# The first batch element of a graph network on one core: its loads over three queues, y plus x on VectorE, layer three's weights folded sooner

## The chip, the cores and the metric

The kernel runs on one core of one Trainium2 chip. The metric is the device time of one execution in microseconds (us). The time before is 2398.67 us, the median of three runs (2397.93 to 2399.6).

The engines have short names in the profile: PE is TensorE (PEld its weight loads), DVE is VectorE, ACT is ScalarE, POOL is GpSimd and SP is SyncE, which here only starts transfers. Each engine takes its instructions in its own order and waits at the first one that isn't ready.

## The reference

Sixteen batch elements, each with 1024 nodes of 128 features (`x`) and a dense 1024 x 1024 matrix `adj`. Layer 0 is applied first, then a network of four message layers, each time with a residual and a layer norm:

```python
# layer 0
degree = adjacency_matrix.sum(axis=-1)[:, :, None]
sum_neighbors = jnp.einsum('bid,bij->bjd', embeddings, cost_matrix) / degree
out = jnp.einsum('bnk,dk->bnd', concatenate([embeddings, sum_neighbors]), W) + b
x = _layernorm(x + relu(out))
# one of the four message layers
src_agg = jnp.einsum('bjv,bij->biv', nodes @ ws + bs, _l2norm(adj, 2))
dst_agg = jnp.einsum('bjv,bji->biv', nodes @ wd + bd, _l2norm(adj, 1))
upd = jnp.concatenate([src_agg, nodes @ wn + bn, dst_agg], axis=2)
nodes = jnp.tanh(upd @ wu + bu)
# after the four layers
x = _layernorm(x + nodes)
```

Both matrices of layer 0 are `adj`. Layers three and four also take the stashed results of earlier layers. `_l2norm` divides the rows (2) or the columns (1) of the matrix by their root of summed squares.

## The kernel before, in words

The order of every engine is written out by hand in the source (a manual schedule over the five engines); a loop over the batch elements holds the layers, and small functions called between the products of a layer (its hooks, numbered by the product that they stand ahead of) prepare what comes next. While one element is computed, the next one's matrix is loaded and its layer 0 computed alongside. The first element has no predecessor, so its loads and its layer 0 stand ahead of the loop, in an order of their own. The change edits only this part and the hooks of the first element's first message layer.

The first element goes as follows. Names and lines are those of the kernel before.

- *Loads.* `load_nodes` (L1056) brings one half of x in four transfers, `load_pair` (L1052) two of the eight row blocks of the matrix, 1 MB, in four transfers (one for each group of 32 partitions). SP takes groups 0 and 1 and GpSimd groups 2 and 3, x first, then the four pairs in the order of `PAIRS`; half 1 of the rows comes ahead of half 0. `w0n` and `b0c` are layer 0's weights and bias. `fetch_weights` (L187 to L192) brings a message layer's three weight matrices `ws`, `wd`, `wn`, its update matrix `wu` and four bias vectors; `load_rows` (L640) brings the matrix once more, in quarters by rows, for the transposed copy `at`. All of these are issued by SP. The order is: weights of layers one and two, row quarter 2, layer three, row quarter 3, layer four, row quarters 0 and 1.
- *Layer 0.* `to_xT` transposes x (L1094), `weights_of_x` multiplies it with W's first half (L1154), and `with_x` (L1163) starts the sum y + x in PSUM with a product of x and the identity. For each row block ScalarE forms squares (`square`, L1114), VectorE the row sum (`degree`, L1120) and TensorE two gather products (`gather`, L1127); GpSimd adds the squares up (`add_square`, L1117). `degree_row` turns the inverse degrees into a row (`dinv`, L359 and L1147), `scaled` (L1150) divides by them, `weights_of_agT` (L1157) finishes y, ScalarE applies the relu (L1158), and `with_y` (L1169) adds y to the sum in PSUM. `norm_stats` (L470 to L481) forms mean and variance on VectorE and the power `rs` on GpSimd; `norm_write_act` and `norm_write` (L490, L486) write x1, and `to_x1` (L1174, L1175) transposes it.
- *Weights.* The update matrix is multiplied into the message weights. `fold_begin` transposes the three matrices (L205, copies L206) and forms the biases (L209, L211, copies L215 to L218); `fold_end` forms the products (L227, copies L229 and L230). Layers one and two are folded inside layer 0, layers three and four by hooks of the first message layer: layer three at hooks 5 and 8, with sums of its weights (L148 to L155) in hook 11.
- *First message layer.* `messages` forms the products of x1 (`pt`, L247) with their additions on VectorE (L698); `row_factors0` forms the row factors `rinv`, and ScalarE scales the row quarters by them (L647); VectorE transposes these into `at` (L655), and `cinv0` makes the row of column factors `cinv` (L359, L351), by which `scale_columns` (L414) scales the matrix. `plain_layer` runs the products `z` and `d` (L851).

TensorE multiplies float32 in two passes: a product in the source is two matmuls in the profile; a transpose is one.

Of the kernel before, what the change touches and what calls it, by code (L numbers as in the profile page):

```python
# [14 lines left out]
P = 128  # L15
NL = 4
CHUNKS = [1, 1, 2, 3]
G = 4
# [5 lines left out]
def adj_resnorm_kernel(ctx: ExitStack, tc: tile.TileContext, x, adj, w0, b0, layers, out):  # L24
# [152 lines left out]

        return wm if l in PAIRED else wm[:, :KEPT[l] * 2 * P].rearrange("p (c v) -> p c v", v=2 * P)

    def fetch_weights(raw, l, q, wm=None):  # L180
        ws, bs, wd, bd, wn, bn, wu, bu = layers[l]
        nch = CHUNKS[l]
        size = max(3 * nch * P, KEPT[l] * 2 * P, WIDTH[l])
        flat = raw.take(size) if wm is None else wm[:, WIDTH[l]:]
        wr = flat[:, :3 * nch * P].rearrange("p (k c v) -> p k c v", k=3, c=nch)
        for k, w in enumerate((ws, wd, wn)):
            q.dma_start(wr[:, k], w.rearrange("(c p) v -> p c v", p=P))  # L187
        wur = raw.take(3 * P).rearrange("p (k v) -> p k v", k=3)
        q.dma_start(wur, wu.rearrange("(c p) v -> p c v", p=P))
        bc = raw.take(4)  # L190
        for k, v in enumerate((bs, bd, bn, bu)):
            q.dma_start(bc[:, k:k + 1], v.rearrange("(p o) -> p o", o=1))  # L192
# [48 lines left out]
    def small(name, shape=(K,)):  # L241
        return ps_s.tile([P, *shape], F32, tag="small", name=name)
# [806 lines left out]
    def load_pair(q, pair, groups):  # L1049
        h, k = pair  # L1050
        for g in groups:
            q.dma_start(a[g * C:(g + 1) * C, h * BPH + k:h * BPH + k + 2], av[h][g, :, k:k + 2])  # L1052

    def load_nodes(q, h, groups):
        for g in groups:
            q.dma_start(xn[g * C:(g + 1) * C, h * BPH:(h + 1) * BPH], xv[h][g])  # L1056

    nc.sync.dma_start(w0n, w0)
    shares = ((nc.sync, range(G // 2)), (nc.gpsimd, range(G // 2, G)))
    for h in (1, 0):  # L1060
        for q, groups in shares:
            load_nodes(q, h, groups)
    make_identity(nc, ident)
    for pair in PAIRS:
        for q, groups in shares:
            load_pair(q, pair, groups)
    nc.sync.dma_start(b0c, b0.rearrange("(p o) -> p o", o=1))
# [29 lines left out]
    pt = small("w0tr", [HW])  # L1097
    for k in range(2):
        nc.tensor.transpose(pt[:, k * P:(k + 1) * P], w0n[:, k * P:(k + 1) * P], ident)
    nc.scalar.copy(w0T.rearrange("p k v -> p (k v)"), pt[:, :2 * P])  # L1100

    sq = []
    for p in (3, 4):
# [9 lines left out]
    def square(i):  # L1113
        nc.scalar.activation(sq[i], a[:, i, :], AF.Square, accum_out=cols[:, i:i + 1])  # L1114

    def add_square(i):
        nc.gpsimd.tensor_add(sq[4], sq[4], sq[i])  # L1117
# [53 lines left out]
    def to_x1(h):  # L1171
        pt = product(f"x1tr_{h}")
# [11 lines left out]
    nc.vector.tensor_add(sq[6], sq[6], sq[7])  # L1184
    add_square(5)
    add_square(6)
# [26 lines left out]
    fold_end(0, fetched[0])  # L1213
    stats[0] = norm_stats(pn[0], range(BPH), "0_0_0")
    root_inverses(cols, inv, slice(NB))
    add_square(second)
    biases = fold_begin(1, fetched[1], nc.vector.tensor_copy, True)
    for q in range(BPH):
        norm_write_act(x1n[:, BPH + q], pn[1][:, q], stats[1], q)
# [17 lines left out]
    for b in range(B):  # L1237
# [8 lines left out]
        if b == 0:  # L1246
# [4 lines left out]
                for q in (2, 3):  # L1251
                    scale_rows(rows[q], q, rinv)

            t = messages(b, 0, feats, wm, {0: lambda: to_x1(0), 2: row_factors0}, with_sums=False)
            cinv = {}

            def columns0(rows, h, engine=nc.vector):
# [2 lines left out]
            def rows0(destination, finish):  # L1260
                for q in (2, 3):
                    transpose_rows(rows[q], q, at)

            def cinv0(destination, finish):
                cinv[0] = factor_rows_now(0, 1, inv, "cinv")

            def second0(destination, finish):
                columns0(range(NJ, NB), 1)
                sums_of_weights(2, fetched[2][3])
                weight_sums(own_seven(2, fetched[2][3]))  # L1270
                nc.sync.dma_start(wsave[2], fetched[2][3])
                destination(1, cinv[0])
                columns0(range(NJ), 1)

# [19 lines left out]
            def folded(l, part):  # L1294
                return lambda *_: part(l, fetched[l])

            hooks = {4: lambda *_: inverses(0, st0, NB), 5: folded(2, fold_begin), 6: rows0, 7: cinv0,
                     8: folded(2, fold_end), 9: lambda *_: fold_and_scale(3, 0), 11: second0, 12: folded(3, fold_end),
                     14: lambda *_: scale_rows(rows[1], 1, rinv), 18: first0, 26: sums0}
            T = combined(0, "T")  # L1300
            plain_layer(b, 0, feats, t, wm, a, at, f1, "acc", hooks)
# [353 lines left out]
```

## Time and profile before

| | |
|---|---|
| median of three runs | 2398.67 us (2397.93 to 2399.6) |
| the profiled execution's own time | 2397.22 us |
| its span, first to last instruction | 2395.3 us |
| TensorE busy | 2377.4 us, 99% of the span |
| VectorE busy | 2088.5 us, 87% |
| ScalarE busy | 977.2 us, 41% |
| GpSimd busy | 273.8 us, 11% |
| moved by DMA | 232.02 MB, 97 GB/s on average |
| granted TensorE clock | 0.999 of full speed |

A profile shows one execution. The time of a run lies 1.9 us above the span here, for what comes before the first and after the last instruction. Busy shares are averages over the whole span; for a change to one stretch the timeline of that stretch is read. It lists, for each engine, when a run of like instructions starts, how long it is busy, the line of the source, the operation with its output and inputs by the program's names, and in brackets how long the engine had been idle and what ended that. "issue" there means that nothing in the profile ended it; at a matmul it can be a transfer.

### The profile page before, as it was taken

Reading aid. Unit: us, or ns where it says so; the run is one execution under the profiler, and the core shown is the slowest. Engines: PE = TensorE matmul, PEld = TensorE weight load, DVE = VectorE, ACT = ScalarE, POOL = GpSimd, SP = SyncE. Lnnn points to the kernel's source line nnn. Section 1 sums busy time; section 2 is a strip of 40 time slices with the busy share of each in tenths; the row PEclk is TensorE's granted clock in tenths of the full one; section 3 lists DMA queues with packets and bytes.
Section 4 is the critical chain, followed back from the end, with each engine's and each line's share of the span. In section 5 each row is a group of like instructions: output and inputs, shape, how many; then the busy total and the mean of one; then the engine's idle time right before and its main releaser. Section 6 shows DMA issues by size and latency. Waiting matters only on the chain.

```text
span 2395.3 us, 39279 instructions
## 1 busy us (share of the span) xinstructions
PE 2377.4 (99%) x15293; PEld 1195.3 (50%) x15293; DVE 2088.5 (87%) x2799; ACT 977.2 (41%) x1827; POOL 273.8 (11%) x102
## 2 busy tenths in 40 slices
PE   8999999999999999999999999999999999999998
PEld 4444464454645446454454554546445464554644
DVE  5998888989889989889988889888898988998954
ACT  5524344253343534435244452434425344352322
POOL 4101111001111011110111110111100111101110
PEclk9999999999999999999999999999999999999999
DMA  9527344262533627235272443624427253362400
GB/s 201 128 75 147 69 114 90 71 147 57 138 75 81 137 48 160 58 97 115 55 163 57 106 97 71 147 69 109 93 69 151 57 133 77 79 142 48 100 22 22
DMA packets 365897, 232.02 MB, mean 97 GB/s; under 512 B 152785, under 2 KB 336849, under 8 KB 365713
## 3 DMA queue, kind: packets, MB, share of 16 engines
q1 hardware_dynamic: 364944, 227.16, 42.5%
q0 software_dynamic: 768, 2.36, 0.4%
q8 instruction: 121, 1.98, 0.4%
q14 instruction: 64, 0.52, 0.1%
HBM read 209.59 MB, written 19.84 MB: 96 GB/s over the span
## 4 chain that ended last, share of the span: by engine, by line
PE 95%; DVE 2%; DMA 1%; SPq 1%; issue 0%; ACT 0%; POOLq 0%; DVEq 0%; ACTq 0%
PE m L1005 39%; PE z L1005 29%; PE pt L247 9%; PE m_f L583 5%; PE pt_z L247 5%; PE z_f L583 2%; PE pw L247 2%; PE m3s L1005 1%; PE z L851 1%; DMA wm<-in_L_gnn_ws_dram 1%; PE pt_p L247 1%; SPq L640 0%; DVE acc L331 0%; DMA raw<-in_L_gnn_wu_dram 0%; DMA a<-in_adj_dram 0%
## 5 line engine op out<-in xcount | busy, mean ns | idle before, releaser
L1005 PE MATMUL m<-a,t 128*64 128x512 f32 x1008 | 432.3, 593 | 0.2 <-DVE t L711 0.2
L1005 PE MATMUL m<-at,t 128*64 128x512 f32 x1008 | 417.3, 593 | 0.0
L1005 PE MATMUL m<-Q,S 128*64 128x512 f32 x880 | 394.0, 593 | 0.0
L1005 PE MATMUL m<-T,S 128*64 128x512 f32 (+1 forms) x1040 | 393.0, 573 | 0.0
L456 POOL TENSOR_TENSOR rs<-ve,mhalf 128x32 f32<-128x32 f32 x30 | 191.9, 6395 | 987.9 <-DVE ve L454 987.9
L1005 PE MATMUL z<-at,t 128*64 128x512 f32 x504 | 229.2, 592 | 0.0
L1005 PE MATMUL z<-at,S 128*64 128x512 f32 x504 | 228.3, 593 | 0.0
L1005 PE MATMUL z<-a,S 128*64 128x512 f32 x504 | 228.2, 593 | 0.0
L1005 PE MATMUL z<-a,t 128*64 128x512 f32 x504 | 227.2, 593 | 0.0
L1005 PE MATMUL z<-Q,t 128*64 128x512 f32 x504 | 227.0, 593 | 0.0
L1005 PEld LDWEIGHTS m<-T,S 128*64 128x64 f32 x1040 | 134.2, 137 | 127.9 <-issue 121.5
L1005 PEld LDWEIGHTS m<-a,t 128*64 128x64 f32 x1008 | 133.6, 137 | 123.5 <-issue 110.9
L1005 PEld LDWEIGHTS m<-at,t 128*64 128x64 f32 x1008 | 135.9, 137 | 112.6 <-issue 107.5
L1005 PEld LDWEIGHTS m<-Q,S 128*64 128x64 f32 x880 | 118.2, 137 | 121.8 <-issue 118.6
L884 ACT COPY e<-m 64x512 f32<-64x512 f32 x63 | 36.6, 581 | 335.9 <-PE m L1005 335.5
L1005 PE MATMUL z<-T,t 128*64 128x512 f32 x384 | 172.8, 592 | 0.0
L376 POOL TENSOR_TENSOR inv<-cols,mhalf 128x16 f32<-128x16 f32 (+1 forms) x17 | 46.8, 2751 | 1031.9 <-DVE cols L375 1031.9
L414 DVE TENSOR_TENSOR a<-a,cinv 128x512 f32<-128x512 f32 x250 | 154.1, 692 | 1.6 <-ACT cinv L351 1.3
L322 ACT ACTIVATE sq<-a 128x1024 f32<-128x1024 f32 x120 | 125.9, 1050 | 35.9 <-DVE acc L329 22.5
L247 PE MATMUL pt<-wm,f1T 128*64 128x128 f32 (+1 forms) x1536 | 126.0, 309 | 0.0
L317 ACT ACTIVATE a<-a 128x1024 f32<-128x1024 f32 x120 | 125.2, 1045 | 0.4
L247 PEld LDWEIGHTS pt<-wm,f1T 128*64 128x64 f32 x1536 | 100.0, 137 | 39.2 <-issue 18.7
(300 smaller groups left out, 4891.9 us busy)
## 6 DMA issues: line engine op xcount, KB each, us to landing
a<-in_adj_dram SPq DMA_DIRECT2D x120, 512.0 KB, 12.9
rows<-in_adj_dram SPq DMA_DIRECT2D x480, 64.0 KB, 2.2
a<-in_adj_dram SPq DMA_DIRECT2D x240, 128.0 KB, 3.5
wm<-wsave SPq DMA_DIRECT2D x32, 704.0 KB, 5.0
wm<-wsave SPq DMA_DIRECT2D x31, 320.0 KB, 3.3
xn<-in_x_dram SPq DMA_DIRECT2D x124, 64.0 KB, 5.5
xs<-in_x_dram SPq DMA_DIRECT2D x60, 128.0 KB, 3.6
cinv<-dr SPq DMA_DIRECT2D x30, 256.0 KB, 6.3
```

What stands on the lines that cost most here:

```text
L247: nc.tensor.matmul(out[s], x[:, s], y, start=start, stop=stop)
L317: nc.scalar.activation(a[:, i, :], a[:, i, :], AF.Copy, accum_out=degree)
L322: nc.scalar.activation(sq, a[:, i, :], AF.Square, accum_out=state["cols"][:, i:i + 1])
L376: nc.gpsimd.tensor_tensor(inv[:, s], cols[:, s], mhalf[:, s], ALU.pow)
L414: engine.tensor_mul(a[:, i, s], a[:, i, s], cinv[:, s])
L456: nc.gpsimd.tensor_tensor(rstd, ve, mhalf[:, :n], ALU.pow)
L583: nc.tensor.matmul(o, x_, y_, start=start, stop=stop)
L851: nc.tensor.matmul(nodes(o) if len(y.shape) == 4 else o, x_, y, start=start, stop=stop)
L884: nc.scalar.copy(e0[high], A[high])
L1005: nc.tensor.matmul(o, x, y_, start=start, stop=stop)
```

## The change

Six things are edited, all in the first element:

- x is loaded by ScalarE's queue, half 1 first and half 0 behind two blocks of the matrix; the four pairs of row blocks are spread over SP, GpSimd and ScalarE; `w0n` follows SP's first two blocks. All bias vectors, `b0c` and those of the four message layers, are loaded by GpSimd's queue (`qb`).
- VectorE clears a tile `idle`, and TensorE forms three products of zeros with it ahead of everything else.
- The transposes of x and W and the products with x stand between the gathers instead of ahead of them.
- y is transposed into PSUM and VectorE adds x to it, into `x1n`, which the norm then reads and writes in place; before, four products added y to a product of x and the identity.
- The weights of layer three are loaded ahead of row quarter 2 instead of behind it (those of layer four ahead of quarter 3); `fold_begin` of layer three stands ahead of the loop, `fold_end` between the message products, and the sums of its weights in hook 6.
- x1's first half is transposed after layer two's fold instead of ahead of it, and the second square of the last pair is formed after the second half of y.

The edits word for word, shortened where lines only move:

```diff
-            q.dma_start(bc[:, k:k + 1], v.rearrange("(p o) -> p o", o=1))
+            (qb or q).dma_start(bc[:, k:k + 1], v.rearrange("(p o) -> p o", o=1))
...
+    idle = one.tile([P, HW], F32, tag="S2", name="idle")
+    nc.vector.memset(idle, 0.0)
+    load_nodes(nc.scalar, 1)
+    load_pair(nc.sync, 0, (0, 1))
+    load_pair(nc.gpsimd, 0, (2,))
+    make_identity(nc, ident)
+    load_pair(nc.scalar, 0, (3,))
     nc.sync.dma_start(w0n, w0)
-    shares = ((nc.sync, range(G // 2)), (nc.gpsimd, range(G // 2, G)))
-    for h in (1, 0):
-        for q, groups in shares:
-            load_nodes(q, h, groups)
-    make_identity(nc, ident)
-    for pair in PAIRS:
-        for q, groups in shares:
-            load_pair(q, pair, groups)
-    nc.sync.dma_start(b0c, b0.rearrange("(p o) -> p o", o=1))
+    load_pair(nc.gpsimd, 1, (2, 3))
+    load_pair(nc.sync, 1, (0,))
+    load_pair(nc.scalar, 1, (1,))
+    load_nodes(nc.scalar, 0)
+    load_pair(nc.scalar, 2, (3,))
+    load_pair(nc.gpsimd, 2, (1, 2))
+    load_pair(nc.sync, 2, (0,))
+    load_pair(nc.gpsimd, 3, (2,))
+    load_pair(nc.scalar, 3, (3,))
+    load_pair(nc.sync, 3, (0, 1))
+    nc.gpsimd.dma_start(b0c, b0.rearrange("(p o) -> p o", o=1))
...
-    for l, q in enumerate((None, 2, 3, None)):
-        fetched.append(fetch_weights(raw, l, nc.sync, None if l else wm))
+    for l, q in enumerate((None, None, 2, 3)):
+        fetched.append(fetch_weights(raw, l, nc.sync, None if l else wm, nc.gpsimd))
...
+    pt = product("idle")
+    for _ in range(3):
+        nc.tensor.matmul(pt, idle[:, :P], idle, start=True, stop=True)
...
     def with_x(h):
-        pn[h] = ps_t.tile([P, BPH, P], F32, tag="pt", name=f"yn0_{h}")
-        nc.tensor.matmul(pn[h].rearrange("p q d -> p (q d)"), ident, xn[:, h * BPH:(h + 1) * BPH].rearrange("p q d -> p (q d)"),
-                         start=True, stop=False)
-    def with_y(h):
+        pt = ps_t.tile([P, BPH, P], F32, tag="pt", name=f"yn0_{h}")
         for q in range(BPH):
             i = h * BPH + q
-            nc.tensor.matmul(pn[h][:, q], yT[:, i * P:(i + 1) * P], ident, start=False, stop=q == BPH - 1)
+            nc.tensor.transpose(pt[:, q], yT[:, i * P:(i + 1) * P], ident)
+        pn[h] = x1n[:, h * BPH:(h + 1) * BPH]
+        nc.vector.tensor_add(pn[h], pt, xn[:, h * BPH:(h + 1) * BPH])
...
-    for h in (1, 0):
-        to_xT(h)
-        with_x(h)
-        weights_of_x(h)
-    for pair in PAIRS[:2]:
-        squares_of(*pair)
-        gathers_of(*pair)
+    to_xT(1)
+    squares_of(*PAIRS[0])
+    gathers_of(*PAIRS[0])
+    transposes_of_w0()
+    squares_of(*PAIRS[1])
+    gathers_of(*PAIRS[1])
+    weights_of_x(1)
+    to_xT(0)
...
     squares_of(*PAIRS[2])
     gathers_of(*PAIRS[2])
+    weights_of_x(0)
...
     square(first)
-    square(second)
     gather(0, second)
     add_square(first)
-    with_y(1)
     scaled(0)
+    with_x(1)
     weights_of_agT(0)
     stats = {1: norm_stats(pn[1], range(BPH), "0_0_1", True)}
+    square(second)
     fold_begin(0, fetched[0])
-    with_y(0)
+    with_x(0)
...
-    to_x1(1)
     biases()
     fold_end(1, fetched[1])
+    to_x1(1)
     for q in range(BPH):
-        norm_write(x1n[:, q], pn[0][:, q], stats[0], q)
+        norm_write(pn[0][:, q], pn[0][:, q], stats[0], q)
+    fold_begin(2, fetched[2])
...
+            def second_x1():
+                to_x1(0)
+                fold_end(2, fetched[2])
...
             def rows0(destination, finish):
                 for q in (2, 3):
                     transpose_rows(rows[q], q, at)
+                sums_of_weights(2, fetched[2][3])
+                weight_sums(own_seven(2, fetched[2][3]))
+                nc.sync.dma_start(wsave[2], fetched[2][3])
```

More of the change, by code (lines that the diff above doesn't have):

```diff
@@ L178, in as_chunks, with fetch_weights @@
         return wm if l in PAIRED else wm[:, :KEPT[l] * 2 * P].rearrange("p (c v) -> p c v", v=2 * P)
-    def fetch_weights(raw, l, q, wm=None):
+    def fetch_weights(raw, l, q, wm=None, qb=None):
         ws, bs, wd, bd, wn, bn, wu, bu = layers[l]
@@ L1047, in adj_resnorm_kernel, with load_pair, load_nodes @@
     PAIRS = [(h, k) for h in (1, 0) for k in range(0, BPH, 2)]
-    def load_pair(q, pair, groups):
-        h, k = pair
+    def load_pair(q, i, groups):
+        h, k = PAIRS[i]
         for g in groups:
             q.dma_start(a[g * C:(g + 1) * C, h * BPH + k:h * BPH + k + 2], av[h][g, :, k:k + 2])
-    def load_nodes(q, h, groups):
-        for g in groups:
+    def load_nodes(q, h):
+        for g in range(G):
             q.dma_start(xn[g * C:(g + 1) * C, h * BPH:(h + 1) * BPH], xv[h][g])
-    nc.sync.dma_start(w0n, w0)
-    shares = ((nc.sync, range(G // 2)), (nc.gpsimd, range(G // 2, G)))
-    for h in (1, 0):
-        for q, groups in shares:
-            load_nodes(q, h, groups)
-    make_identity(nc, ident)
-    for pair in PAIRS:
-        for q, groups in shares:
-            load_pair(q, pair, groups)
-    nc.sync.dma_start(b0c, b0.rearrange("(p o) -> p o", o=1))
+    idle = one.tile([P, HW], F32, tag="S2", name="idle")
[5 more added lines that the diff above has]
+    load_pair(nc.scalar, 0, (3,))
+    nc.sync.dma_start(w0n, w0)
+    load_pair(nc.gpsimd, 1, (2, 3))
[9 more added lines that the diff above has]
+    nc.gpsimd.dma_start(b0c, b0.rearrange("(p o) -> p o", o=1))
     raw = Raw()
@@ L1095, in to_xT, with transposes_of_w0 @@
         nc.scalar.copy(nodes(xT[:, half(h)]), blocks(pt))
[L1097 to L1100, printed above, removed]
+    pt = product("idle")
+    for _ in range(3):
+        nc.tensor.matmul(pt, idle[:, :P], idle, start=True, stop=True)
+    def transposes_of_w0():
+        pt = small("w0tr", [HW])
+        for k in range(2):
+            nc.tensor.transpose(pt[:, k * P:(k + 1) * P], w0n[:, k * P:(k + 1) * P], ident)
+        nc.scalar.copy(w0T.rearrange("p k v -> p (k v)"), pt[:, :2 * P])
     sq = []
@@ L1218, in adj_resnorm_kernel @@
     for q in range(BPH):
-        norm_write_act(x1n[:, BPH + q], pn[1][:, q], stats[1], q)
-    to_x1(1)
+        norm_write_act(pn[1][:, q], pn[1][:, q], stats[1], q)
     biases()
     fold_end(1, fetched[1])
+    to_x1(1)
     for q in range(BPH):
-        norm_write(x1n[:, q], pn[0][:, q], stats[0], q)
+        norm_write(pn[0][:, q], pn[0][:, q], stats[0], q)
+    fold_begin(2, fetched[2])
     kept = scratch.tile([N, D], F32, tag="kept", name="kept0")
@@ L1252, in row_factors0 @@
                     scale_rows(rows[q], q, rinv)
-            t = messages(b, 0, feats, wm, {0: lambda: to_x1(0), 2: row_factors0}, with_sums=False)
+            def second_x1():
+                to_x1(0)
+                fold_end(2, fetched[2])
+            t = messages(b, 0, feats, wm, {0: second_x1, 2: row_factors0}, with_sums=False)
             cinv = {}
@@ L1268, in second0 @@
                 columns0(range(NJ, NB), 1)
-                sums_of_weights(2, fetched[2][3])
-                weight_sums(own_seven(2, fetched[2][3]))
-                nc.sync.dma_start(wsave[2], fetched[2][3])
                 destination(1, cinv[0])
@@ L1295, in folded @@
                 return lambda *_: part(l, fetched[l])
-            hooks = {4: lambda *_: inverses(0, st0, NB), 5: folded(2, fold_begin), 6: rows0, 7: cinv0,
-                     8: folded(2, fold_end), 9: lambda *_: fold_and_scale(3, 0), 11: second0, 12: folded(3, fold_end),
+            hooks = {4: lambda *_: inverses(0, st0, NB), 6: rows0, 7: cinv0,
+                     9: lambda *_: fold_and_scale(3, 0), 11: second0, 12: folded(3, fold_end),
                      14: lambda *_: scale_rows(rows[1], 1, rinv), 18: first0, 26: sums0}
```

## The prediction

> **What bounds the kernel now.** I read the page first, for the share that the change can reach. Two lines carry it:
>
> ```profile
> span 2395.3 us, 39279 instructions
> ...
> PE   8999999999999999999999999999999999999998
> ```
>
> The row PE gives TensorE's busy share in 40 slices of 59.9 us. Only the first and the last slice hold idle TensorE time; the change edits the first element, which is the first slice. All it can win is what TensorE loses there, and what follows is shifted as a whole. So I read that slice instruction by instruction in the timeline (start, duration, engine, line, operation, and in brackets the idle time before it and what ended it).
>
> ```profile
> 13.28 0.30 PEld L1127 LDWEIGHTS pa<-a,xn 128*128 128x128 f32 x2 [2.90 <-issue]
> 13.29 1.06 ACT L1114 ACTIVATE sq<-a 128x1024 f32<-128x1024 f32 x1 [3.26 <-DMA a<-in_adj_dram]
> 13.30 2.35 DVE L1120 TENSOR_REDUCE cols<-a 128x1 f32<-128x1024 f32 x2 [8.20 <-DMA a<-in_adj_dram]
> ...
> 18.87 1.22 DVE L1184 TENSOR_TENSOR sq<-sq,sq_row 128x1024 f32<-128x1024 f32 x1
> ...
> 20.00 0.17 DVE L1124 RECIPROCAL inv<-cols 128x4 f32<-128x4 f32 x1
> ...
> 20.29 0.41 PEld L359 LDWEIGHTS dinv<-ident,inv 128*128 128x128 f32 x4 [0.70 <-issue]
> ```
>
> TensorE, ScalarE and VectorE all start on the matrix at 13.3 us, when the first pair of row blocks (1 MB) has landed. From there the gathers run at 0.43 us a pass, 16 passes for two pairs, and the third pair waits at 20.29 for a chain that ends on ScalarE: squares, sum of two squares on VectorE, reciprocal, transposes (`dinv`). The same view of GpSimd:
>
> ```profile
> 8.41 0.53 POOL L1052 DMA_DIRECT2D a<-in_adj_dram  x1 [0.50 <-DMA xn<-in_x_dram]
> ...
> 15.57 2.36 POOL L1117 TENSOR_TENSOR sq<-sq,sq 128x1024 f32<-128x1024 f32 x1 [6.51 <-ACT sq L1114]
> 20.24 2.37 POOL L1117 TENSOR_TENSOR sq<-sq,sq 128x1024 f32<-128x1024 f32 x1 [2.31 <-DVE inv L1124]
> 22.75 2.37 POOL L1117 TENSOR_TENSOR sq<-sq,sq_x 128x1024 f32<-128x1024 f32 x1
> ...
> 30.15 2.35 POOL L1117 TENSOR_TENSOR sq<-sq 128x1024 f32<-128x1024 f32 x1 [2.60 <-ACT sq L1114]
> 32.61 1.04 POOL L479 TENSOR_TENSOR rs<-ve,mhalf 128x4 f32<-128x4 f32 x1
> ```
>
> GpSimd is done with its DMAs at 8.9 us, adds five squares with waits between, and then takes the powers for the layer norm (`rs`), on which x1 and everything after it hangs. Last, the stretch where layer three's weights are folded:
>
> ```profile
> 41.76 6.49 ACT L647 ACTIVATE Q<-Q,rinv 128x256 f32<-128x256 f32 x16 [2.73 <-DMA Q<-in_adj_dram]
> ...
> 48.67 0.71 PE L209 MATMUL bm<-raw 128*128 128x128 f32 x4 [0.71 <-ACT raw L206]
> ```
>
> TensorE's bias product waits for a copy that stands behind 6.5 us of row scaling on ScalarE. From 62.24 us on TensorE goes on without a gap.
>
> **The Trainium skill.** "DMA: Bandwidth & Descriptors", Issuing engines are not separate DMA queues: transfers from SP, ScalarE and GpSimd run on the same 16 engines, and spreading them saves issue time alone. The trace agrees for the bound: by stretches the DMA share is 0.95 to 1.07 from 3 to 21 us. The rate isn't constant, though: 223 GB/s at 6 to 9 us and 318 at 12 to 15, when both queues had matrix rows in flight, so a third queue may help a little. "TensorE: Matmul & The Clock Gate", The HAM clock gate, has TensorE at half clock until about 3.4 us of sustained work. The trace agrees: 0.83 us between the first passes at 6.56 and 7.39, 0.43 at 13.8 (the granted-clock row doesn't show it). Nothing else here needs a page.
>
> **The change part by part.**
>
> *Arrival.* x half one now comes on ScalarE's queue, pair 0 on three queues, x half zero behind pair 1. Ahead of the last piece of pair 0 stand 0.26 MB of x, 1.05 of matrix, 0.13 of w0 and some 0.3 of GpSimd's next blocks: 1.7 MB from 1.8 us at 250 GB/s (between the two rates above) is 8.5 us, against 13.28: a gain of 4.8 for TensorE and VectorE (7.5 to 9.5).
>
> *What it costs on ScalarE.* In the program's order ten DMAs now stand ahead of ScalarE's first computing instruction. In the built program the loads of SP and ScalarE share eight semaphores, and an issue waits for the load eight places before it (before, SP alone had them: its ninth after w0, b0c, goes at 7.85). ScalarE's last (pair 3) waits for pair 1's group 0; SP holds that one until pair 0's last group, ScalarE's own, has landed (8.5). From issue to landing a block of this size took 4.7 us at least, so it lands at 12.7 to 13.2, and ScalarE starts computing at about 13.2 (11.5 to 15). Queued there: the table load (1.28, done at 0.73 under the wait before), the x copy 0.5, four squares at 1.1 (4.4), the w0 copy 0.35: the fourth square ends at 19.7, before at 18.8. VectorE's sum 1.13, the reciprocal and the transposes follow as before: `dinv` at 21.1 instead of 20.29. So the 4.8 us are lost: +0.8.
>
> *TensorE in the gathers.* The x products of both halves, the w0 transposes and half zero's transposes ran before 13.28, in the wait. Now they stand between the gathers. Those ahead of `dinv` lie in its wait. The second x product (2 x 0.43 = 0.86) lies between pair 2 and pair 3: +0.8. The first y (L1158, 28.29) comes at 29.9.
>
> *The zero products* (6 passes, at half clock 0.85 each, 5.1 us from about 1.5) end at 6.6, before pair 0; they cost nothing and give the gathers at 8.5 the full clock. Without them the first 3.4 us of gathers, 4 passes instead of 8, would lose 1.7 us, all within the wait for `dinv`: nothing.
>
> *y plus x.* The two products with x (2 x 0.86) go, in the old wait: nothing. y's 8 passes (0.97) become 4 transposes (0.55): -0.4; VectorE adds 0.69 and a semaphore's 0.1 per half: +0.8. Norms from SBUF instead of PSUM: 0.27 and 0.34 a piece before; I take no change (a tenth less each would give 0.1 to 0.3). Statistics at 32.2 instead of 30.23 (+2.0 in all); the powers could start at 34.6 instead of 32.61. Half zero's y moves ahead of the last square: it takes 1.05 off that half, which waits for half one anyway.
>
> *Biases on GpSimd.* Seventeen 0.5 KB loads leave SP (some 0.45 each, 7.7 us), and layer three's four loads (0.6 MB, 3 us at 200 GB/s) go ahead of the first rows: about even for the rows, whose scaling waits for `rinv` at 41.7. They now stand ahead of GpSimd's additions, with eight semaphores of their own: the seventh bias load waits for b0, which is queued behind six matrix blocks. These (1.57 MB at a third to a half of 310 GB/s) land by 17 to 18.5, b0 at 18.5; then eight issues at 0.55 (a row of 128 pieces took 0.55): GpSimd is free at 22.5 (21 to 26), not 8.9. Five additions at 2.45 end at 34.7. Before they were hidden in waits; now they end with the statistics (34.6), the cover is gone, and each further us is one on the path. `rs`: +2.0.
>
> *Layer three's fold.* Its six transposes, biases and twelve products stood at 46.71 to 49.33 and 52.47 to 54.12: 2.6 and 1.65 with their stall, together 4.3. They go between x1's halves, where TensorE waits for copies. But there ScalarE has four copies (1.2) ahead of x1's first half now, and its first part is ahead of the message products: these start at 36.73 + 2.0 + 1.2 + 0.8 (what the x1 copy doesn't hide) = 40.7; the second part delays the rest by 1.5. z (L851, 42.31) comes at 47.8, +5.5. Taking back 4.3: +1.2. The row scaling starts 5.5 later; the copies of `cinv`, behind it, end at 55 instead of 52.9. VectorE's nine sums of layer three's weights (2.4 us) move from behind its first column scaling to ahead of it, the same work before `e` (58.37). VectorE comes out some 2 us late against 2.1 us of waits it has at 66 and 74: nothing, but with no cover left.
>
> *Sum:* 0.8 + 0.8 + 0.4 to `rs`, then + 3.5 - 4.3: **+1.2 us**, up to 1.7 with late semaphores; I take **+1.5**. The profiled execution took 2397.2 us, its span 2395.3 and 1.9 around it; it becomes 2398.7. The runs' median stood 1.5 above it: **2400.2**.
>
> **Rivals.** *GpSimd becomes the bound* (slower): if b0 and the seventh load land late, or issue costs more than 0.55, the additions end after the statistics. For: 17 loads and 12 us of additions are now in one row ahead of `rs`. Against: tiny loads, with a queue whose big blocks leave early. From 22.4 us on each us counts; at 27 it is 1.5 + 4.5 = +6. It passes 0.2% (4.8 us, about what a measurement of this kernel can tell) from 26 us.
> *The arrival gain gets through* (faster): ScalarE is free at 8 to 10.5, because blocks land in 2.5 us on three queues. Then `dinv` is at 18.5 to 16, GpSimd is free at 19, and the sum is -0.7 to -3.6; SP's wait for ScalarE's block speaks against it.
> *The change doesn't do what it says:* the DMA engines serve the queues so that x, in small pieces, starves behind the matrix, and pair 0 lands at 11 to 13: ScalarE at 16, +4.
>
> **Numbers.** Near even 0.58; GpSimd 0.20, of which 0.15 above 4.8; starved x 0.08, of which 0.05 above; gain through 0.14, of which 0.05 below -4.8, as the bound -3.6 could be off by the unshown rate. Faster 0.05, same 0.75, slower 0.20. Range -3.7 to +6.3: 2395 to 2405.
>
> **What would show it.** Gathers start at 8 to 9; ScalarE's table load at 12 to 14 after its last DMA; `dinv` near 21; GpSimd's first addition at 22 to 23 and no wait until `rs` at 34 to 35; z at 47 to 48; no L205 to L230 between it and `cinv`; the gapless run from 63.5. Wrong: table load before 10, additions after 26, or a time beyond 2395 to 2405.

## The result, and the profile after

The changed kernel takes 2403.97 us (median of 10 runs, 2402.77 to 2405.03), the kernel before 2397.76 us beside it: a ratio of 1.0026, 95% interval 1.0017 to 1.0035. It is 6.2 us slower. The forecast range of 2395 to 2405 holds that, at its edge: counted from the kernel before it ended at +6.3. It is in part luck that it does. The likeliest case (+1.5 us) is not what happened: two rivals on the slow side came in part, together, with about 3.3 us each, where GpSimd alone had been priced at +6. The profiled execution took 2404.49 us, its span is 7.1 us longer than before:

```profile
span 2402.4 us, 39279 instructions
...
PE   8999999999999999999999999999999999999998
```

The row is the same to the digit, so it shows no new idle time further on; the stretches below place the loss in the first 70 us. In the timeline, the lines that answer to those shown of before (start, duration, engine, line, operation; in brackets the idle time and what ended it):

```profile
10.17 1.08 PE L1103 MATMUL xtr<-ident,xn 128*128 128x128 f32 x4 [3.53 <-DMA xn<-in_x_dram]
...
12.25 5.75 PE L1141 MATMUL pa<-a,xn 128*128 128x512 f32 x8 [1.00 <-DMA a<-in_adj_dram]
...
15.90 1.28 ACT L1104 ACT_TABLE_LOAD   x1 [15.90 <-DMA a<-in_adj_dram]
...
22.24 1.22 DVE L1197 TENSOR_TENSOR sq<-sq,sq_row 128x1024 f32<-128x1024 f32 x1 [3.88 <-ACT sq_row L1128]
23.38 0.17 DVE L1138 RECIPROCAL inv<-cols 128x4 f32<-128x4 f32 x1
...
23.70 0.62 PE L359 MATMUL dinv<-ident,inv 128*128 128x128 f32 x4 [0.70 <-DVE inv L1138]
...
32.52 0.69 ACT L1172 ACTIVATE yT<-pw,b0c 128x512 f32<-128x512 f32 x1 [1.13 <-PE pw L1171]
```

x, asked for first, comes at 10.1 us; pair 0 at 12.2, one microsecond sooner than before, not five. ScalarE starts computing at 15.90, and `dinv` follows at 23.70 (20.32 before). The last line is the first y. TensorE's eight passes for pair 0 take 5.75 us; at 0.43 us a pass they would take 3.5. Below, TensorE is called cold where its passes take up to twice the 0.43 us (half clock), and warm where they take 0.43. GpSimd in the same view:

```profile
8.18 0.54 POOL L192 DMA_DIRECT2D raw<-in_L_gnn_bd_dram  x1 [1.80 <-DMA a<-in_adj_dram]
11.68 0.54 POOL L192 DMA_DIRECT2D raw<-in_L_gnn_bn_dram  x1 [2.95 <-DMA a<-in_adj_dram]
...
27.53 0.54 POOL L192 DMA_DIRECT2D raw<-in_L_gnn_bu_dram  x1
28.07 0.12 POOL L1097 MEMSET inv<- 128x8 f32 x1
28.14 4.78 POOL L1131 TENSOR_TENSOR sq<-sq,sq 128x1024 f32<-128x1024 f32 x2
...
37.87 2.35 POOL L1131 TENSOR_TENSOR sq<-sq 128x1024 f32<-128x1024 f32 x1
40.17 1.04 POOL L479 TENSOR_TENSOR rs<-ve,mhalf 128x4 f32<-128x4 f32 x1
```

From the second to the seventh bias vector of the message layers, each issue waits for a matrix block (11.1 us of waits in all), and two later ones wait for an earlier bias vector (2.5 us); the additions start at 28.14, run without a gap, and `rs` comes behind the last, at 40.17 (32.61 before). For the fold, TensorE's lines after; the last of them follows its last wait, 0.66 us ahead of the gapless stretch:

```profile
43.64 1.48 PE L205 MATMUL wtr<-ident,raw 128*128 128x128 f32 x6
...
48.27 1.50 PE L227 MATMUL wm<-raw 128*128 128x128 f32 x12
...
53.77 1.98 PE L851 MATMUL z<-x_T,wm 128*128 128x512 f32 x4
...
69.40 0.94 PE L227 MATMUL wm<-raw 128*128 128x128 f32 x6 [0.20 <-ACT wx L230]
```

and in the kernel before the first y, z and the same last line:

```profile
28.29 0.69 ACT L1158 ACTIVATE yT<-pw,b0c 128x512 f32<-128x512 f32 x1 [1.14 <-PE pw L1157]
...
42.31 1.98 PE L851 MATMUL z<-x_T,wm 128*128 128x512 f32 x4
...
61.58 0.94 PE L227 MATMUL wm<-raw 128*128 128x128 f32 x6 [0.20 <-ACT wx L230]
```

So the gapless stretch starts 7.82 us later (70.06 against 62.24). By stretches (before / after):

| from | to | before | after | difference |
|---|---|---|---|---|
| 0 | `dinv` | 20.32 | 23.70 | +3.38 |
| `dinv` | first y | 7.97 | 8.82 | +0.85 |
| first y | `rs` | 4.32 | 7.65 | +3.33 |
| `rs` | z | 9.70 | 13.60 | +3.90 |
| z | TensorE's last wait | 19.27 | 15.63 | -3.64 |

The span grew by 0.7 us less than this; that much lies in the rest of the run, and I have not traced it. The medians differ by another 0.9 less: the profiled execution of before lay 0.5 us below the median, that of after 0.5 above it.

### The profile page after: what moved, and what is told of

Read it like the earlier page. It is cut to its first block, busy times and chain, and to the rows that moved or that the text cites. A ratio compares the mean times of both kernels' runs of the same rounds, so it can differ in the third digit from the quotient of the medians.

```text
span 2402.4 us, 39279 instructions
## 1 busy us (share of the span) xinstructions
PE 2382.7 (99%) x15287; PEld 1196.7 (50%) x15287; DVE 2090.4 (87%) x2802; ACT 977.4 (41%) x1827; POOL 280.6 (12%) x113
## 4 chain that ended last, share of the span: by engine, by line
PE 95%; DVE 2%; DMA 1%; POOL 1%; issue 1%; ACT 1%; POOLq 0%; DVEq 0%; ACTq 0%
PE m L1005 39%; PE z L1005 29%; PE pt L247 9%; PE m_f L583 5%; PE pt_z L247 5%; PE z_f L583 2%; PE pw L247 2%; PE m3s L1005 1%; PE z L851 1%; DMA a<-in_adj_dram 1%; PE pt_p L247 1%; PE d L851 0%; POOL sq L1131 0%; DMA raw<-in_L_gnn_bd_dram 0%; DVE acc L331 0%
## 5 line engine op out<-in xcount | busy, mean ns | idle before, releaser
L884 ACT COPY e<-m 64x512 f32<-64x512 f32 x63 | 36.6, 582 | 335.9 <-PE m L1005 335.5
```

Source lines behind the costliest of these rows:

```text
L884: nc.scalar.copy(e0[high], A[high])
```

## The experiments

Each was timed beside the kernel before, which gave 2396.67 to 2396.92 us there and 2397.76 beside the changed kernel; the difference stands in brackets behind the time. So a time of an experiment against that of the changed kernel has about 1 us of doubt. "Gapless" is the start of TensorE's gapless stretch, its last wait plus 0.66.

The columns of starts are one profile each. With the same loads of x and matrix, the first gathers start at 12.81 to 13.72 (before, e3, e5 to e7) and at 11.02 to 12.28 (after, e1, e4, e8, e10); a shift of less than about 1 us between two runs there shows nothing. The two groups lie 1.6 us apart in the mean.

| run | first gathers | `dinv` | `rs` | gapless | time | ratio to before |
|---|---|---|---|---|---|---|
| before | 13.31 | 20.32 | 32.61 | 62.24 | | |
| after | 12.25 | 23.70 | 40.17 | 70.06 | 2403.97 (+6.21) | 1.0026 [1.0017, 1.0035] |
| e1 biases on SP | 11.38 | 23.45 | 36.60 | 66.24 | 2400.40 (+3.59) | 1.0015 [1.0008, 1.0021] |
| e2 no loads on ScalarE | 12.11 | 23.19 | 36.74 | 66.33 | 2401.01 (+4.20) | 1.0018 [1.0010, 1.0025] |
| e3 loads of before | 13.13 | 24.03 | 37.17 | 66.80 | 2401.68 (+4.87) | 1.0021 [1.0012, 1.0030] |
| e4 fold of before | 11.08 | 23.47 | 39.81 | 72.37 | 2406.80 (+9.99) | 1.0042 [1.0028, 1.0056] |
| e5 e3 and order of before | 13.72 | 22.36 | 34.63 | 64.27 | 2398.27 (+1.35) | 1.0004 [0.9996, 1.0012] |
| e6 e3 and longer zeros | 13.19 | 21.65 | 34.78 | 64.42 | 2399.23 (+2.31) | 1.0007 [0.9999, 1.0016] |
| e7 before and early fold | 12.81 | 19.9 | 32.18 | 61.90 | 2397.06 (+0.14) | 0.9999 [0.9991, 1.0007] |
| e8 no zeros | 11.02 | 23.27 | 39.76 | 68.57 | 2404.45 (+7.53) | 1.0030 [1.0019, 1.0042] |
| e9 three repairs | 13.03 | 23.07 | 36.21 | 65.86 | 2399.30 (+2.51) | 1.0009 [1.0001, 1.0017] |
| e10 two repairs | 12.28 | 23.81 | 36.97 | 66.60 | 2400.90 (+4.11) | 1.0016 [1.0010, 1.0023] |
| e11 before, single blocks | 10.90 | 19.08 | 31.38 | 61.00 | 2395.08 (-1.71) | 0.9992 [0.9983, 1.0000] |
| e12 e11 and inverse first | 11.08 | 17.94 | 30.22 | 60.44 | 2395.07 (-1.60) | 0.9992 [0.9984, 1.0001] |

**e1, the biases.**

```diff
-    nc.gpsimd.dma_start(b0c, b0.rearrange("(p o) -> p o", o=1))
+    nc.sync.dma_start(b0c, b0.rearrange("(p o) -> p o", o=1))
...
-        fetched.append(fetch_weights(raw, l, nc.sync, None if l else wm, nc.gpsimd))
+        fetched.append(fetch_weights(raw, l, nc.sync, None if l else wm))
```

> The changed kernel with all seventeen bias loads back on SP's queue, everything else as changed. Theory G (GpSimd is the bound at the power `rs`, because its bias loads hold its additions until 28.1 us): the additions start at about 23 with waits between them, `rs` comes right after the variances, at about 37.8 instead of 40.17, and the time falls by 2.3 us. Rival S (ScalarE, held by its own DMAs until 15.9 us, sets the statistics, and GpSimd would have been in time): `rs` moves by less than 0.5 us and the time stays within 0.5 us of the changed kernel's. If SP's queue suffers from the seventeen loads, the row quarters land later and the scaling of the rows (53.2 us) shows it, not `rs`.

`rs` came 3.57 us sooner and the time is 3.57 lower (2.6, counted from the kernel before beside each). The additions began at 19.70 instead of the 23 expected. In GpSimd's timeline of e1 the last addition waits for its square again, and `rs` follows it:

```profile
34.14 2.36 POOL L1131 TENSOR_TENSOR sq<-sq 128x1024 f32<-128x1024 f32 x1 [3.47 <-ACT sq L1128]
36.60 1.04 POOL L479 TENSOR_TENSOR rs<-ve,mhalf 128x4 f32<-128x4 f32 x1
```

From first y (32.28) to `rs` it is 4.32 us, exactly as before. So GpSimd's bias loads were a bound of 3.3 to 3.6 us. That it is exactly as before has a reason: in both kernels `rs` starts 0.1 us after the end of GpSimd's last addition, which had waited for a square that ScalarE forms right behind the first y (before: 30.15 + 2.35 = 32.50, `rs` at 32.61). GpSimd's order, not the statistics, sets `rs` there. Theory G named the mechanism; it expected 2.3, because it left the variances where the changed kernel had them (`ve` ready at 37.8). They came sooner too; why is the last section. `rs` stays 4 us late, as `dinv` does not move.

**e2, ScalarE's loads.** All `nc.scalar` in the load section became `nc.sync`; these are twelve loads (the prediction counts ten, the expectations fourteen).

```diff
-    load_nodes(nc.scalar, 1)
+    load_nodes(nc.sync, 1)
...
-    load_pair(nc.scalar, 0, (3,))
+    load_pair(nc.sync, 0, (3,))
```

> The changed kernel with ScalarE's fourteen loads issued by SP in the same places of the order; biases stay on GpSimd. Theory S: the table load comes before 11 us instead of 15.9, the fourth square ends near 19, `dinv` at about 20.5 instead of 23.70, the statistics at about 31.5 instead of 34.77. Theory G: GpSimd still has its bias loads ahead of the additions, which start at 28 as before, so `rs` stays near 40 and the time falls by less than 1 us although the statistics come 3 us sooner. If S alone is right, `rs` falls to 37 and the time by 3 us.

The table load came at 0.74 and the fourth square ended at 21.1, but `dinv` gained only 0.5 us. Theory S fell in this form. Nor was GpSimd as late as I assumed for it: with SP's order changed its additions began at 24.5, ran without a gap and ended at 36.6, just ahead of `rs`; that is where the 3 us came from. So `rs` and the time came near what was expected if S alone were right, for another reason. What holds `dinv` here stands in TensorE's timeline of e2:

```profile
12.11 6.29 PE L1141 MATMUL pa<-a,xn 128*128 128x512 f32 x8 [4.57 <-DMA a<-in_adj_dram]
18.24 0.38 PE L1113 MATMUL w0tr<-ident,w0n 128*128 128x128 f32 x2
18.46 3.60 PE L1141 MATMUL pa<-a,xn 128*128 128x512 f32 x8
...
23.19 0.60 PE L359 MATMUL dinv<-ident,inv 128*128 128x128 f32 x4
```

There is no wait from 12.11 to `dinv`: TensorE itself is the bound, though a narrow one (`inv` was ready 0.7 us earlier, at 22.46), with eight passes at half clock and then W's transposes, an x product and x transposes in between.

**e3, all loads as before.** This is the load section of the kernel before, with layer three's weights still ahead of row quarter 2.

```diff
-    load_nodes(nc.scalar, 1)
-    load_pair(nc.sync, 0, (0, 1))
...
+    nc.sync.dma_start(w0n, w0)
+    for q, groups in shares:
+        load_nodes(q, 1, groups)
...
+    for i in range(4):
+        for q, groups in shares:
+            load_pair(q, i, groups)
```

> The changed kernel with the load section of the kernel before (x, matrix and biases on SP and GpSimd, none on ScalarE), but layer three's weights still ahead of row quarter 2; the zero products, the order of the gathers, y plus x on VectorE and the early fold stay. If the loads are the whole loss (S and G together): `dinv` at 20.5 to 21, `rs` at 33 to 34, the gapless stretch starts at 62 to 63.5, and the time is 6 to 8 us below the changed kernel's, within 1.5 us of the kernel before. Rival F (the early fold of layer three costs by itself, since z moved by 11.5 us while `rs` moved by 7.6): the gapless stretch starts at 66 or later, and the time stays 3 us or more above the kernel before.

The first expectation failed. Rival F has the number, with the gapless stretch at 66.80, but not the cause, since the loss is there at `dinv` already, ahead of the fold. `dinv` was at 24.03, later than in the changed kernel: TensorE's passes for pair 0 took 6.11 us, and on ScalarE the copy of W's transposes, queued ahead of pair 1's squares, waited 4.19 us for TensorE.

**e4, the fold as before.**

```diff
-    for l, q in enumerate((None, None, 2, 3)):
+    for l, q in enumerate((None, 2, 3, None)):
...
-    fold_begin(2, fetched[2])
...
-                fold_end(2, fetched[2])
...
+            hooks = {4: lambda *_: inverses(0, st0, NB), 5: folded(2, fold_begin), 6: rows0, 7: cinv0,
+                     8: folded(2, fold_end), 9: lambda *_: fold_and_scale(3, 0), 11: second0, 12: folded(3, fold_end),
```

> The changed kernel with layer three's weights loaded, folded and summed where the kernel before does it; the changed loads stay. Theory F: the time falls by 3 us or more. Theory L (only the loads cost, the fold is even, as 4.3 us of TensorE time are put in ahead and taken out behind): `rs` stays at 40, z comes at about 50 instead of 53.8, the gapless stretch starts at 69 to 71 and the time is within 1.2 us of the changed kernel's.

It became slower, by 2.8 us (3.8, counted from the kernel before beside each); the gapless stretch starts 2.3 us later. In the wait for `rs` TensorE stood nearly idle and came out cold: in e4 the four transposes of x1 took 1.51 us and the first 24 message passes 1.97 and 3.27, in the kernel before 1.04, 1.08 and 1.95. In the changed kernel a part of this half-clock time falls on the fold's transposes (1.48 us for six; 0.98 in e7). So with a late `rs` the early fold helps, if not by less work.

**e5 and e6, TensorE in the gathers.** e5 puts the order of before on top of e3; e6 only lengthens the zero products of e3.

```diff
# e5
-    to_xT(1)
-    squares_of(*PAIRS[0])
...
+    transposes_of_w0()
+    for h in (1, 0):
+        to_xT(h)
+        weights_of_x(h)
+    for pair in PAIRS[:2]:
+        squares_of(*pair)
+        gathers_of(*pair)
# e6
-    for _ in range(3):
+    for _ in range(10):
         nc.tensor.matmul(pt, idle[:, :P], idle, start=True, stop=True)
```

> The kernel with the loads of before (label e3), and now also the order of before ahead of the gathers: transposes of W and x and both products with x come first, and nothing but gathers stands between pair 0 and `dinv`. Left of the change are the zero products, y plus x on VectorE and the early fold. Theory T (with the loads undone, TensorE itself set `dinv` at 24.03: its first 8 gather passes ran at half clock, 6.1 us instead of 3.5, because it had been idle since 6.2, and 1.5 us of products and transposes stood between): the first 8 passes take 3.5 us, `dinv` starts at 20.3 to 20.6, the first y at 28.3 to 28.7, `rs` at 32.6 to 33.1, the gapless stretch at 61.5 to 62.2, and the time is 3.5 to 4.5 us below e3's, within 1 us of the kernel before. Rival V (y plus x on VectorE costs what is left, 3 to 4 us between y and `rs`): `dinv` improves but `rs` stays at 35 or later.

> The kernel of e3 (loads of before, changed order) with ten zero products instead of three, 20 passes instead of 6, so that TensorE is busy until about 12 us. Theory T, the part of the clock: the first 8 gather passes then take 3.5 us instead of 6.1, `dinv` starts near 21.6 instead of 24.03, `rs` at 34.7 instead of 37.17, and the time falls by 2.5 us against e3. If the order alone is the loss and the clock isn't, the gathers still take 6 us and nothing moves.

TensorE's timeline of e6:

```profile
13.19 3.67 PE L1135 MATMUL pa<-a,xn 128*128 128x512 f32 x8 [0.99 <-issue]
...
21.65 0.60 PE L359 MATMUL dinv<-ident,inv 128*128 128x128 f32 x4
```

All of e6 came as expected: seven more zero products, work of no use, took 2.4 us off `dinv` and off `rs`, and 2.45 off the time. What is left in e6 is the moved work itself: its first gathers start as before and are warm, yet `dinv` is 1.33 us later than before and the stretch from there to the first y 0.83 longer, together all but 0.02 of the 2.18 us by which its gapless stretch is late. e5 took the 1.5 us of other work out of the way and gained 3.4 us of time, but its gathers were cold again (8.80 us for 16 passes, 7.10 before), so `dinv` came at 22.36 and not at 20.3 to 20.6; theory T's number failed by those 1.7 us. From first y (30.30) to `rs` e5 has 4.33 us, so rival V falls: y plus x on VectorE costs nothing there, as GpSimd's last addition ends later than the statistics need.

**e7, the fold alone**, in the kernel before:

```diff
+    fold_begin(2, fetched[2])
...
+            def second_x1():
+                to_x1(0)
+                fold_end(2, fetched[2])
```

> The kernel before with only layer three's fold moved (weights loaded ahead of row quarter 2, first part ahead of the loop, second part between the message products, sums of its weights in hook 6). Theory E (even: in e1, e2 and e3 the stretch from `rs` to z grew by 3.7 us against before and that from z to the gapless stretch shrank by 3.6): `rs` at 32.6, z near 46, gapless from 61.2 to 62.0, time within 0.6 us of before. Rival P (as I forecast: it costs 1.2 us more than it takes back): gapless from 62.6 or later. Rival W (e4, where undoing it cost 2.8 us, carries over): gapless from 59.5 or sooner, and the time 2 us or more below before.

It is even: from `rs` to z +3.72 us, from z to the last wait -3.63, time the same. Theory E holds.

**e8, no zero products.**

```diff
-    nc.vector.memset(idle, 0.0)
...
-    for _ in range(3):
-        nc.tensor.matmul(pt, idle[:, :P], idle, start=True, stop=True)
```

> The changed kernel without the three zero products and the tile that VectorE clears for them. Theory T: they do nothing for the gathers, since TensorE idles for 3.5 us behind them and the granted clock falls to 0.5 to 0.6 before pair 0 arrives; the gathers of pair 0 take 5.7 to 6.1 us as before, and the time stays within 0.7 us of the changed kernel's. Rival: they had shortened the half-clock stretch, and without them the gathers take 1 us more and `dinv` comes later by as much.

The time stayed within 0.5 us (1.3, counted from the kernel before beside each), with overlapping intervals. The passes of pair 0 took 6.71 us, 1 more than with zeros, as the rival said, but they started earlier and `dinv` came no later, since it waits for `inv`. The three products show neither help nor harm.

**e9 and e10, the causes together.** Both have e1's edit and nine zero products; e9 also e2's.

> The changed kernel with three things put right at once: all biases on SP's queue, ScalarE's loads issued by SP in the same places, and nine zero products (18 passes) instead of three, so that TensorE stays warm until the matrix arrives. Each of the first two alone gave 3 us, because behind it the other, or TensorE at half clock, set `dinv` at 23.2 to 23.7. If there are these three causes and no fourth: pair 0 is there at about 12.1, the first 8 gather passes take 3.5 us, `dinv` starts at 20.5 to 21, the first y at 29.3 (0.9 us of x product still stands behind pair 2), `rs` at 33.6, the gapless stretch at 62.5, and the time is 6 to 7 us below the changed kernel's, 0.5 to 1.5 above before. If ScalarE's loads weren't a cause, it is no better than label e10.

> The changed kernel with biases on SP and nine zero products, but ScalarE's fourteen loads left where they are. If ScalarE, held by its loads until 15.7 us, is a cause of its own: the gathers run at full clock and end sooner, but `dinv` still waits for the inverses on VectorE, at 23.2 to 23.5 as in e1 (23.45), `rs` at 36.5, time as in e1, 3 us above e9. If only the clock held the chain in e1, `dinv` falls to 20.5 to 21 and the time by 2.5 us against e1.

TensorE in e10, then in e9:

```profile
23.81 0.62 PE L359 MATMUL dinv<-ident,inv 128*128 128x128 f32 x4 [1.96 <-DVE inv L1138]
```

```profile
18.27 3.67 PE L1141 MATMUL pa<-a,xn 128*128 128x512 f32 x8 [1.35 <-DMA a<-in_adj_dram]
...
23.07 0.60 PE L359 MATMUL dinv<-ident,inv 128*128 128x128 f32 x4
```

e10 shows ScalarE's loads as a cause of their own: its gathers are warm (3.67 us), TensorE is through early and waits 1.96 us for `inv`, whose squares on ScalarE start at 17.79. But e9 gained far less than expected, 1.6 us of time over e10: pair 1 landed only at 18.2, and TensorE waited 1.35 us for it. The products moved between the gathers are still there too, with the 1.3 us that e6 shows. So there is a further cause, how the loads are ordered and shared between the queues; no run parts these two. The views by stretches show it (start and end, length, busy time of five engines with counts, then granted clock, DMA share, GB/s); first before, then after:

```profile
9.00:12.00 3.00, 2.21 (x8) 0.74 (x6) 0.00 (x0) 0.58 (x1) 0.05 (x1) 1.00 1.04 298
12.00:15.00 3.00, 1.69 (x4) 0.87 (x5) 1.70 (x2) 1.71 (x3) 0.00 (x0) 1.00 1.03 318
```

```profile
9.00:12.00 3.00, 1.08 (x4) 0.71 (x4) 0.00 (x0) 0.00 (x0) 0.32 (x1) 0.60 1.02 206
12.00:15.00 3.00, 2.75 (x4) 1.23 (x5) 2.35 (x2) 0.00 (x0) 0.70 (x2) 0.50 1.07 214
```

At the same DMA share the changed kernel moves a third less, and its granted clock falls to 0.5 to 0.6. In these two stretches e9, which has the changed order without ScalarE's queue, moves 257 and 255 GB/s (e2: 256 and 244), e1, with that queue but without the biases, 217 and 203, e3, with the loads of before, 288 and 332. The groups stay apart in every profile: the five with the loads of before move 275 to 298 and 305 to 341, the five with three queues 206 to 221 and 203 to 215. So the biases aren't what lowers the rate; the order and the third queue each have a part.

**e11 and e12, a version meant to beat both.** From the first gather to y TensorE has hardly a gap in the kernel before, so an earlier first gather should carry through to y; half a megabyte is enough for it.

```diff
# e11, on the kernel before
-        for g in groups:
-            q.dma_start(a[g * C:(g + 1) * C, h * BPH + k:h * BPH + k + 2], av[h][g, :, k:k + 2])
+        for r in (k, k + 1):
+            for g in groups:
+                q.dma_start(a[g * C:(g + 1) * C, h * BPH + r:h * BPH + r + 1], av[h][g, :, r:r + 1])
# e12, on e11
+    degree_inverses(1)
     nc.vector.tensor_add(sq[6], sq[6], sq[7])
     add_square(5)
     add_square(6)
-    degree_inverses(1)
```

> A version meant to beat both: the kernel before, with each row block of the matrix loaded by itself (sixteen more transfers of half the size on SP and GpSimd), so that gathers and squares of the first block can start when 0.5 MB of matrix has landed instead of 1 MB. From the first gather to y TensorE has hardly a gap in before, so what the first gather gains y gains, as long as the following blocks come at least as fast as TensorE's 1.7 us for a block: gathers from 11.7 instead of 13.3, `dinv` at 19.2 instead of 20.3, `rs` at 31.5 instead of 32.6, time 1 us lower, at the edge of what shows in the total. Rival: the smaller transfers lower the rate, or the issues behind one another (0.55 us each on GpSimd) delay the later blocks; then `dinv` stays at 20 or later.

> The kernel of e11 (before, with each row block loaded by itself) with one exchange in VectorE's order: the reciprocal of the degrees (`inv`) now ahead of the sum of two squares, which it doesn't need. In e11 that sum ran from 15.82 for 3.02 us, beside GpSimd's addition, and `dinv` waited 1.15 us for `inv` behind it. If that sum is what holds `dinv`: it starts right behind the 16 gather passes, near 18.0 instead of 19.08, y and `rs` come 1.1 us sooner (`rs` at 30.3), and the time is 2.5 to 3 us below before. Rivals: the third pair's blocks land no sooner than 19, or GpSimd's addition behind the later sum holds `rs`; then the time is e11's.

e11 is 1.7 us below before; the interval of its ratio reaches from a gain of 0.17% to none, so the total alone doesn't settle it. The profile shows where it comes from: gathers at 10.90, `dinv` and `rs` 1.2 us sooner. The first gather starts 2.4 us sooner (the block had landed by 9.8, when ScalarE squares it; TensorE was still at the products with x), of which `dinv` keeps half, since it waits for `inv` behind VectorE's sum:

```profile
10.90 7.03 PE L1128 MATMUL pa<-a,xn 128*128 128x512 f32 x16
...
15.82 3.02 DVE L1185 TENSOR_TENSOR sq<-sq,sq_row 128x1024 f32<-128x1024 f32 x1
...
19.08 0.62 PE L359 MATMUL dinv<-ident,inv 128*128 128x128 f32 x4 [1.15 <-DVE inv L1125]
```

e12 takes that wait away: `dinv` at 17.94, right behind the gathers, `rs` at 30.22. But the gapless stretch gains only 0.56 us more and the time nothing. ScalarE's row scaling, ahead of layer three's copies, now waits in its middle for a transfer:

```profile
43.15 3.30 ACT L647 ACTIVATE Q<-Q,rinv 128x256 f32<-128x256 f32 x8 [0.49 <-DMA raw<-in_L_gnn_ws_dram]
```

## Why the prediction was right or wrong

The sum said +0.8 +0.8 +0.4 to `rs` and then -0.8, taken as +1.5. Measured: +7.6 to `rs` and +0.3 after it in the profile, +6.2 in the medians. The sum is wrong ahead of `rs`, where it has +2.0; behind it, it is nearly right.

- *Arrival, 8.5 us: wrong, 12.2* (11.0 to 12.3 in the five profiles with these loads). Both terms were mis-sized. The rate was not 250 GB/s but 213 to 220 from 3 to 9 us and 206 behind it. And by 12.24 some 2.2 MB had moved (0.24 + 0.64 + 0.66 + 0.68 by stretches), not the 1.7 that I put ahead of pair 0's last piece. The third rival is what happened, nearly to its numbers (pair 0 at 11 to 13, ScalarE at 16, +4): x starved behind the matrix. The median from issue to landing of a transfer of x was 9.0 us on ScalarE's queue, 2.3 and 3.2 before on SP's and GpSimd's. "DMA: Bandwidth & Descriptors", Queues, rings and completion order, says that each DMA engine takes turns among the queues packet by packet. That fits a queue of 512-byte pieces beside two of 4 KB. In e2, with x in SP's queue ahead of SP's matrix blocks, its transposes start at 6.74 instead of 10.17; but e2 also has a queue less, so no run here isolates the turns.
- *ScalarE, 13.2: the right kind of wait, 2.7 us too early.* It did wait for a matrix block at its last loads, but all blocks came later than forecast: SP's own matrix issues were drawn out to 19.0 us. e10 shows this cause alone: `inv` is late by 1.96 us for a warm TensorE.
- *"Those ahead of `dinv` lie in its wait": the step that failed most quietly.* The transposes and x product between the gathers were costed at nothing because TensorE was to wait for ScalarE. e2 took ScalarE's delay away and `dinv` stayed: TensorE was as late as ScalarE, at half clock and with 1.5 us of extra work. Two causes of 3 us each lay beside one another, so that undoing either showed almost nothing at `dinv`. The moved work alone, with warm gathers, costs 1.3 us there (e6), where the prediction has nothing.
- *Zero products: right that they cost nothing (e8), wrong that they give the gathers full clock.* They end at 6.64; then TensorE waits 3.53 us for x. "TensorE: Matmul & The Clock Gate", The HAM clock gate, puts an idle window of about 3.4 us as enough for half clock; the granted clock of 0.60 and 0.50 behind that wait agrees, and e6 shows the price, 2.4 us. As a limit it doesn't hold here: in e4 waits of 2.66 and 1.05 us were followed by gathers just as cold (5.98 us for eight passes, granted clock 0.50).
- *Second x product, +0.8: right.* From `dinv` to first y it is +0.85.
- *y plus x, +0.4: right for the statistics, nothing at `rs`.* They begin 2.25 us after first y instead of 1.94; yet from first y to `rs` e1 has 4.32 us, as before. The prediction let the statistics set `rs`; what set it before the change was GpSimd's last addition.
- *GpSimd free at 22.5: wrong, 28.1,* beyond the 26 that the prediction named as a sign of being wrong. The mechanism was as put, with each microsecond on the path, but I let the issues wait only up to the seventh bias load, and that one for b0, where the profile has it wait for a matrix block. The waits for matrix blocks began with the second, the seventh came at 20.23 (18.5 was forecast), and behind it stood nine issues of 0.54 and 2.5 us of waits. The rival priced 27 us at +6; alone it cost 3.3 to 3.6, because the statistics were late as well.
- *Layer three's fold, +5.5 - 4.3: in sum nearly right.* Of the +5.5, 3.5 lay behind `rs`; e7 shows 3.72 and a return of 3.63. The return was over-counted by 0.7, and as a whole the edit is even (+0.1 behind `rs`, where the sum has -0.8).

## What to carry to other kernels

A move that is costed at nothing because it lies in a wait needs that wait to last: ask which engine is next in line if the wait shrinks, and what the moved work and a cold TensorE add to that engine. If undoing a suspect shows nothing, look whether a second cause ends at the same place, and undo both (in e9 a third one showed then). To start earlier on data that is still arriving, try waiting for less of it (e11) before spreading it over more queues.

## What was unexpected of the hardware

- In e11 VectorE's sum of two squares took 3.02 us instead of 1.22; it ran beside GpSimd's addition (15.39 to 17.75). In the changed kernel the variances did the same:

```profile
35.43 2.35 POOL L1131 TENSOR_TENSOR sq<-sq,sq 128x1024 f32<-128x1024 f32 x1
36.50 1.31 DVE L473 TENSOR_SCALAR ve<-mv 128x4 f32<-128x4 f32 x1
```

  This operation on 128 x 4 takes 0.17 us for the other half (40.24); here it ends at 37.81, when GpSimd's addition ends (37.78). The same holds in all fourteen profiles, the kernel before included (0.56 us, to 32.54, against 32.50). "SBUF — State Buffer", SBUF: two separate sides, says that the two engines share one pair of ports, held by one for a whole instruction while the other stands still; on VectorE's side it limits this to instructions with two inputs in SBUF or in a two-port mode. For the sum, with two inputs, the trace agrees. `ve` has one input, and that it runs in such a mode no run here shows. Either way GpSimd without gaps delayed VectorE as well.
- Three queues, in the changed order, moved less than two in the order of before: 206 and 214 GB/s against 298 and 318 in the same stretches, with the DMA engines equally busy, and likewise in the other eight profiles of these two kinds.
- In e5 TensorE idled for only 1.84 us ahead of the gathers, less than the 2.10 before, and was cold nevertheless. Why stays open. Nor does the granted clock show every such stretch: in e8 it reads 1.00 from 9 to 15 us, where the passes of pair 0 took 6.71 us instead of 3.5.
